# A window-attention layer's TensorE order written out part by part, with two smaller reorderings in the layers behind it

## The chip, the core and the metric

The kernel runs on one core of one Trainium2 chip. The metric is the device time of one execution in microseconds; lower is better. The core has TensorE for matrix products, with a weight load ahead of each (the profile lists the two as PE and PEld), VectorE (DVE), ScalarE (ACT), GpSimd (POOL) and SyncE (SP), which here only issues DMA transfers. Each engine takes its instructions in the order of its own queue and waits at semaphores for what other engines have to do first.

## The reference

Eight images of 56 x 56 pixels with 192 channels, in float32, go through four layers of one form: x becomes x + layer(GroupNorm(x)).

- Layer 0 is a gated unit with two Toeplitz products, along the rows and along the columns.
- Layer 1 is shifted-window attention. The image is rolled by 3 pixels and cut into 64 windows of 7 x 7 = 49 pixels. A layer norm is followed by q, k and v; each of 6 heads of 32 channels computes softmax(q k^T / sqrt(32) + bias + mask) v in each window; an output projection follows.
- Layer 2 projects 192 channels to 384, mixes the pixels of every channel with a banded matrix, takes running averages along image directions, and then applies a layer norm and a projection back to 192.
- Layer 3 is a depthwise convolution, a layer norm, and two projections with a hidden layer of 768 channels.

## The kernel before, in words

The kernel treats the layers one after the other, each as one stage or several. In layers 1 to 3 the 192 channels lie as 3 groups (j) of 64 on the partitions, and two halves of the image (s, rows 0 to 27 and 28 to 55) share the 128 partitions. Tile, the layer that the kernel is written in, keeps an order of its own for each engine: a planner reorders instructions within what the data allow, unless the program says otherwise. Three means of saying otherwise occur here: `tc.manual_schedule(engines=...)` keeps the named engines in program order from there to the end of the enclosing block, `tc.keep_in_program_order(...)` keeps single instructions in it, and a buffer count (`bufs`) makes an instruction wait until the older user of the buffer is done.

**Layer 1, units.** An image is worked in 4 units (g): 7 rows of pixels of each half, 8 windows in each half, 392 pixels a half. A unit has these steps, and the names in brackets are those of the profile:

- the projections of q and k (line 677, `qk_ps`): two for q, two for k, each of 6 matmuls into two banks; copied by ACT (683, 685) or DVE (687)
- v (line 697, `v_ps`): two groups of 4 windows, each 48 matmuls into two banks; copied by ACT for half 0 (705) and by DVE for half 1 (707)
- the scores (line 717, `S`): 48 matmuls for each half, into one tile S of three banks; then on DVE the bias (724) and the maximum (726), on POOL the subtraction (727), on ACT the exponential (728), on DVE the sum (730) and its reciprocal (731), on POOL the scaling (732). The result is `e`, in one of two sets
- the mix: 12 transposes of `e` for each half in 3 groups (747, `et_ps`), copied by ACT and DVE in turn (752, 754); 48 matmuls with v (760, `po`), copied by ACT and DVE (771, 773); three projections (779, `pr`), each added to x on DVE (784)

One matmul of float32 data appears as two passes in the profile's counts, so that a group of 48 shows as 96.

PSUM has 8 banks here: three of tag `mm`, shared by qk, v, po, pr and the norm's products, two of tag `et`, and three for S.

**Layer 1, the norm.** `layer1_norm` is a generator for the following image: it scales (ACT, line 636), takes the mean over the channels with a matmul (643), subtracts it (DVE, 645), squares (ACT, 647), sums with a matmul (651), takes the square root (ACT, 652, once per unit on 32 partitions), the reciprocal (DVE, 654), spreads it with a matmul (659) and multiplies (DVE, 661). It hands back control 14 times, and the loop over the units calls it some times for each unit (`plan`).

**Layer 1, order.** In the loop the scores of unit g + 1 are written before the mix of unit g. The planner orders all engines.

**Layer 2's input.** `layer2_image` clears the edge rows of a buffer on POOL (790, 791) and loads an image (793, 794), one of two buffers (`xpool`). `layer2_in` scales it in 3 instructions on DVE (803) into `xn`, POOL clears edges in it (801, 806, 807), and 174 passes on TensorE (815, `pin`) in 15 groups are each taken from PSUM by DVE with the bias (823). Image 0 is loaded by POOL's queue, the following ones by SyncE's.

**Layer 2's output and layer 3's input.** The layer norm's statistics (line 190), scalings (936 on DVE, 938 on ACT), transposes (947, `tp`), the affine part (948, ACT), the projection (960) and the addition to x (965, DVE) of one image lie beside `layer3_in` for the image before: its GroupNorm, transposes of the image (1006, `zps`) in 4 groups for each of 3 channel groups, and copies to `zt`, by DVE (995) and ACT (993) in turn, stored for the depthwise convolution. DVE runs in program order here.

Of the kernel before, what the change touches and what calls it, by code (L numbers as in the profile page):

```python
# [10 lines left out]
F32 = mybir.dt.float32  # L11
# [8 lines left out]
HC = 96  # L20
# [57 lines left out]
def kernel(ctx: ExitStack, tc: tile.TileContext, a: dict, out: bass.AP):  # L78
# [105 lines left out]
    def run(steps):  # L184
        for _ in steps:
            pass
# [435 lines left out]
    def layer1_norm(b, x, pool, psum, consts):  # L622
# [10 lines left out]
        for g in range(4):  # L633
            gs = bass.ts(g, TT)
            for j in range(3):
                nc.scalar.activation(
                    xw[:, j, gs].rearrange("p (w i j) -> p w i j", i=7, j=7),
                    x[:, j, 7 * g:7 * g + 7].rearrange("p i (w j) -> p w i j", j=7), AF.Identity,
                    bias=sh[:, j:j + 1], scale=sc[:, j:j + 1],
                )  # L640
            mp = psum.tile([128, 512], F32, name="mean", tag="mm", bufs=3)[:, 0:TT]
            for j in range(3):
                nc.tensor.matmul(mp, ones2, xw[:, j, gs], start=(j == 0), stop=(j == 2))
            xs = xw[:, :, gs]
            nc.vector.tensor_tensor(xs, xs, mp.unsqueeze(1).to_broadcast([128, 3, TT]), ALU.subtract)
            sq = pool.tile([128, 3, TT], F32, name="sq")
            nc.scalar.activation(sq, xs, AF.Square)
            yield
            vp = psum.tile([128, 512], F32, name="vps", tag="mm", bufs=3)[32 * g:32 * g + 32, 0:TT]
            for j in range(3):  # L650
                nc.tensor.matmul(vp, ones32, sq[:, j], start=(j == 0), stop=(j == 2))
            nc.scalar.activation(rs[32 * g:32 * g + 32], vp, AF.Sqrt, bias=eps5[32 * g:32 * g + 32])
            yield
        nc.vector.reciprocal(rs, rs)
        yield
        for g in range(4):
            gs = bass.ts(g, TT)
            bp = psum.tile([128, 512], F32, name="rstd", tag="mm", bufs=3)[:, 0:TT]
            nc.tensor.matmul(bp, sel[32 * g:32 * g + 32], rs[32 * g:32 * g + 32], start=True, stop=True)
            xs = xw[:, :, gs]  # L660
            nc.vector.tensor_tensor(xs, xs, bp.unsqueeze(1).to_broadcast([128, 3, TT]), ALU.mult)
            yield

    def layer1_scores(g, xr, pool, psum, S, es, consts):
# [5 lines left out]
        qk = [pool.tile([HC, 2, 2, TT], F32, name=f"qk{s}", bufs=1) for s in range(2)]  # L670
        for which in range(2):
            for m in range(2):
                ps = [psum.tile([128, 512], F32, name="qk_ps", tag="mm", bufs=3)[0:HC, 0:TT] for s in range(2)]
                c0 = which * C + m * HC
                for j in range(3):
                    for s in range(2):
                        nc.tensor.matmul(  # L677
                            ps[s], wg[64 * s:64 * s + 64, j, c0:c0 + HC], xw[64 * s:64 * s + 64, j, gs],
                            start=(j == 0), stop=(j == 2),
                        )  # L680
                for s in range(2):
                    if which == 0:
                        nc.scalar.activation(qk[s][:, 0, m], ps[s], AF.Identity, bias=bq[:, m:m + 1])  # L683
                    elif s == 0:
                        nc.scalar.copy(qk[s][:, 1, m], ps[s])
                    else:
                        nc.vector.tensor_copy(qk[s][:, 1, m], ps[s])

        v = [pool.tile([128, 8, HC], F32, name=f"v{s}") for s in range(2)]
        for w4 in range(0, 8, 4):  # L690
            ps = [psum.tile([128, 512], F32, name="v_ps", tag="mm", bufs=3)[:, 0:4 * HC] for s in range(2)]
# [10 lines left out]
            for s in range(2):  # L702
# [3 lines left out]
                else:  # L706
                    nc.vector.tensor_copy(dst, ps[s])
        for s in range(2):
            bm = pool.tile([128, 24, WN], F32, name="bm")
# [22 lines left out]
            nc.gpsimd.tensor_tensor(ev, ev, sm.unsqueeze(2).to_broadcast([128, 24, WN]), ALU.mult)  # L732
        return v

    def layer1_mix(g, x, v, pool, psum, es, consts):

        w_proj, bpr = consts[2:4]
        oa = []
        for s in range(2):
            e = es[g % 2][s]  # L740

            et = pool.tile([128, 12, 128], F32, name="et")
            for i in range(3):
                tp = psum.tile([128, 512], F32, name="et_ps", tag="et", bufs=2)
                for k in range(4):
                    at = 8 * i + 2 * k
                    nc.tensor.transpose(
                        tp[:, 128 * k:128 * k + 128], e[:, at:at + 2].rearrange("p a b -> p (a b)"), ident
                    )
                dst = et[:, 4 * i:4 * i + 4].rearrange("p a b -> p (a b)")  # L750
                if i % 2 == 0:
                    nc.scalar.copy(dst, tp)
                else:
                    nc.vector.tensor_copy(dst, tp)
            o = pool.tile([HC, 2, TT], F32, name=f"oa{s}", bufs=1)
            po = [psum.tile([128, 512], F32, name="po", tag="mm", bufs=3)[0:HC, 0:TT] for _ in range(2)]
# [10 lines left out]
            for hh in range(2):  # L767
# [4 lines left out]
                else:  # L772
                    nc.vector.tensor_copy(dst, src)
            oa.append(o)
        for j in range(3):
            ps = psum.tile([128, 512], F32, name="pr", tag="mm", bufs=3)[:, 0:TT]
# [6 lines left out]
            xs = x[:, j, 7 * g:7 * g + 7].rearrange("p i w -> p (i w)")  # L783
            nc.vector.scalar_tensor_tensor(xs, ps, bpr[:, j:j + 1], xs, ALU.add, ALU.add)


# [10 lines left out]
    def layer2_in(b, x, pool, psum, w_in, b_in):  # L797
# [4 lines left out]
        for j in range(3):  # L802
            nc.vector.tensor_scalar(
                xn[:, j, :, 0:W], x[:, j], sc[:, j:j + 1], sh[:, j:j + 1], ALU.mult, ALU.add
            )
        nc.gpsimd.memset(xn[0:64, :, 0, 0:W], 0.0)
# [161 lines left out]
    def layer3_in(b, x, zp, pool, psum):  # L968
# [21 lines left out]

        def to(dst, src, eng):
            if eng:
                nc.scalar.copy(dst, src)
            else:
                nc.vector.tensor_copy(dst, src)

        for j in range(3):
            zt = pool.tile([OP, 64, NB], F32, name="zt")
            nc.gpsimd.memset(zt[:, :, 0:1], 0.0)
            nc.gpsimd.memset(zt[:, :, NB - 1:NB], 0.0)  # L1000
            for g, m0 in enumerate(range(0, PH + 1, 4)):
                yield
# [10 lines left out]
                dst = bass.AP(dst.tensor, dst.offset, [list(dst.ap[0]), [1, n2], [PH, 2], [NB, 64]])  # L1013
                to(dst, tp[:, 0:n2], g % 2)
                if nm > n2:

                    to(zt[:, :, 1 + 2 * PH], tp[:, n2, 1], 0)
                    to(zt[0:64, :, 1 + PH], tp[0:64, n2, 0], 1)
            nc.sync.dma_start(zd[b][:, 64 * j:64 * j + 64], zt)
# [215 lines left out]
    with ExitStack() as st:  # L1235
# [25 lines left out]
        if nimg > 1:  # L1261
            x.append(layer1_load(1, xpool))
        values = layer1_scores(0, xr[0], pool, psum, S, es, consts)


        plan = [(1, 1, 1), (1, 1, 2), (1, 2, 1), (0, 1, 2)]
        gn = []
        last = slice(nimg - 1, nimg)
        for b in range(nimg):
            gn.append(pool.tile([128, 3, NTH, 6], F32, name="gh_st"))  # L1270
            steps = layer1_norm(b + 1, x[b + 1], pool, psum, consts) if b + 1 < nimg else iter(())
            for g in range(4):
# [6 lines left out]
                if g == 1 and b == nimg - 1:  # L1279
                    run(gn_finish(mv2[:, 0:b], scsh2[:, 0:b, 0], scsh2[:, 0:b, 1], pool, psum, "mm"))  # L1280
                first, second, third = plan[g]
                for _ in range(first):
                    ahead = next(steps, None)
                    if ahead is not None:
                        xr.append(ahead)
                for _ in range(second):
                    next(steps, None)
                following = None
                if g < 3 or b + 1 < nimg:
                    following = layer1_scores((g + 1) % 4, xr[b + (g == 3)], pool, psum, S, es, consts)  # L1290
                for _ in range(third):
                    next(steps, None)
                layer1_mix(g, x[b], values, pool, psum, es, consts)
                values = following
                gn_piece(gn[b], x[b].rearrange("p j h w -> p j (h w)"), g)
                if b + 1 == nimg:
                    rolled_rows(x2[b], x[b], g)
            for _ in steps:
                pass
            if b + 1 < nimg:  # L1300
# [5 lines left out]
    with ExitStack() as st:  # L1306
        xpool = st.enter_context(tc.tile_pool(reuse_waits="tile", name="l2x", bufs=2, side="right"))
        pool = st.enter_context(tc.tile_pool(reuse_waits="tile", name="l2i", bufs=2))
        psum = st.enter_context(tc.tile_pool(reuse_waits="tile", name="l2ip", bufs=4, space=PSUM))
        x = [layer2_image(0, xpool, nc.gpsimd)]  # L1310
        w_in = resident("w_in", nc.scalar, pool)
# [204 lines left out]
```

## Time and profile before

| what | value |
|---|---|
| time before, median of 3 runs (lowest, highest) | 6227.99 us (6226.70, 6247.08) |
| profiled execution: its own time | 6250.54 us |
| profiled execution: span, mean granted TensorE clock | 6248.8 us, 0.925 |
| busy in the span: PE, PEld | 5549.3 us (89%), 3585.7 us (57%) |
| busy in the span: DVE, ACT, POOL | 3450.3 (55%), 2251.5 (36%), 1328.0 (21%) |
| layer 1, from the first `mean` of image 1 to the last `pr` | about 2115 to 3568 us |
| layer 2's input | 3615.67 to 3859 us |
| layer 2's mixing, layer 2's output with layer 3's input | 3883 to 4490 us, 4490 to 5040 us |

Times in the text count from the start of the span of the profiled execution. In a line of groups the columns are the line of the source, the engine, the operation, out<-in by names, the sizes and the count; behind the first bar the busy time and the mean in ns of one; behind the second the idle time of the engine just ahead of these instructions and what ended most of it. A line of the timeline has the start, the length and the group, and in brackets the idle time just before it with what ended it. "Issue" is time in which the engine waited for nothing that the profile shows. The granted clock is a share of full speed.

### The profile page before, as it was taken

The numbers are of one execution on the slowest core, as the hardware profiler recorded it, in microseconds if no ns is written. First come the engines' busy times: TensorE is split into PE (matmuls) and PEld (weight loads), VectorE is DVE, ScalarE is ACT, GpSimd is POOL, SyncE is SP. The second block draws the span as 40 slices with busy tenths as digits, with TensorE's granted clock in tenths as the row PEclk, the third lists the DMA queues.
The fourth block names the chain that finished last, engine by engine and source line by source line (L and its number), as shares of the span: only waits on it lengthen the run. The fifth ranks groups of instructions, "written<-read, shape, count | busy, mean of one in ns | idle before, by whom it ended". The sixth has DMA issues, their size and how long they took to land. (4 is left out here: it accounts for less than half of the span.)

```text
span 6248.8 us, 126609 instructions
## 1 busy us (share of the span) xinstructions
PE 5549.3 (89%) x55636; PEld 3585.7 (57%) x55636; DVE 3450.3 (55%) x4800; ACT 2251.5 (36%) x2932; POOL 1328.0 (21%) x869
## 2 busy tenths in 40 slices
PE   6799989999999888888888688999888889799999
PEld 5577766666666454445444466767544479544444
DVE  5677766556565344444444376888788710433331
ACT  2334444344444233333333200445455510233333
POOL 1100025444444122121212101333300100110100
PEclk8899989999999888878888798999999989899999
DMA  6799986666665515545442586677667579421210
GB/s 165 186 216 214 191 242 255 264 261 258 256 256 213 80 34 60 60 60 56 56 48 41 67 239 226 209 232 239 189 167 208 162 288 331 154 82 64 72 57 24
DMA packets 1034540, 1013.11 MB, mean 162 GB/s; under 512 B 826136, under 2 KB 958196, under 8 KB 1007220
## 3 DMA queue, kind: packets, MB, share of 16 engines
q1 hardware_dynamic: 1019424, 940.93, 54.0%
q0 software_dynamic: 8832, 41.81, 2.2%
q10 hardware_dynamic: 5732, 22.27, 1.1%
q8 instruction: 437, 7.16, 0.5%
q14 instruction: 115, 0.94, 0.0%
HBM read 676.28 MB, written 345.08 MB: 163 GB/s over the span
## 5 line engine op out<-in xcount | busy, mean ns | idle before, releaser
L371 PE MATMUL qv<-w_qv_sb,xn 64*112 64x288 f32 x5376 | 722.1, 425 | 50.3 <-DVE act L377 46.9
L409 POOL COPY lc<-lt 128x896 f32<-128x896 f32 (+1 forms) x320 | 572.1, 1805 | 624.5 <-PE op L417 608.4
L371 PEld LDWEIGHTS qv<-w_qv_sb,xn 64*112 64x112 f32 x5376 | 535.0, 184 | 232.5 <-DVE act L377 63.2
L378 ACT ACTIVATE act<-act 112x576 f32<-112x576 f32 x448 | 299.9, 682 | 462.8 <-DVE act L377 425.8
L1145 PE MATMUL ph<-y,w_sb 64*128 64x392 f32 x2304 | 398.4, 498 | 6.5 <-ACT hid L1149 6.5
L429 PE MATMUL pj<-xn,w_p_sb 64*128 64x392 f32 (+1 forms) x1920 | 374.0, 516 | 14.0 <-issue 10.7
L1156 PE MATMUL po<-hid,w_sb 128*64 128x392 f32 x2304 | 386.3, 494 | 0.0
L417 PEld LDWEIGHTS op<-rc,lc 128*56 128x56 f32 x9216 | 310.6, 137 | 127.2 <-issue 61.8
L417 PE MATMUL op<-rc,lc 128*56 128x56 f32 x9216 | 342.1, 222 | 45.2 <-POOL lc L409 26.1
L450 PE MATMUL y<-pp,w_o_sb 128*64 128x392 f32 (+1 forms) x1920 | 357.3, 505 | 18.9 <-DVE x L458 10.2
L377 DVE TENSOR_TENSOR act<-qv,b_qv 112x576 f32<-112x576 f32 x448 | 320.7, 751 | 85.4 <-PE qv L371 85.0
L1163 DVE TENSOR_TENSOR x<-x,z 128x392 f32<-128x392 f32 x96 | 70.4, 733 | 522.8 <-ACT z L1161 522.8
L409 ACT COPY rc<-rt 128x896 f32<-128x896 f32 (+1 forms) x160 | 256.9, 1606 | 240.6 <-PE op L417 226.7
L727 POOL TENSOR_TENSOR e<-e,mx 128x1176 f32<-128x1176 f32 x64 | 139.9, 2185 | 954.3 <-DVE mx L726 899.4
L866 PE MATMUL cv<-zc,wt 128*128 128x224 f32 x1536 | 313.7, 356 | 24.1 <-DMA zc<-pd 24.1
L866 PEld LDWEIGHTS cv<-zc,wt 128*128 128x128 f32 x1536 | 290.9, 190 | 67.8 <-issue 51.6
L443 DVE TENSOR_TENSOR pp<-pp,ot 128x784 f32<-128x784 f32 (+1 forms) x160 | 154.6, 966 | 306.6 <-ACT pp L434 288.3
L677 PE MATMUL qk_ps<-xr,wg 64*96 64x392 f32 x1536 | 309.7, 512 | 15.1 <-ACT qk L683 13.5
L1145 PEld LDWEIGHTS ph<-y,w_sb 64*128 64x128 f32 x2304 | 220.4, 189 | 176.4 <-issue 26.0
L1046 PE MATMUL cps<-zc,wt 128*128 128x224 f32 x1536 | 299.5, 356 | 18.0 <-DMA zc<-zd 17.6
L1046 PEld LDWEIGHTS cps<-zc,wt 128*128 128x128 f32 x1536 | 289.5, 189 | 27.8 <-issue 20.4
L1156 PEld LDWEIGHTS po<-hid,w_sb 128*64 128x64 f32 x2304 | 162.6, 137 | 213.8 <-issue 213.8
(211 smaller groups left out, 9423.0 us busy)
## 6 DMA issues: line engine op xcount, KB each, us to landing
lt<-left SPq DMA_DIRECT2D x72, 1792.0 KB
rt<-right SPq DMA_DIRECT2D x72, 1792.0 KB
left<-qv SPq DMA_DIRECT2D x224, 252.0 KB
right<-qv SPq DMA_DIRECT2D x448, 126.0 KB
wt<-in_band_dram SPq DMA_DIRECT2D x23, 2048.0 KB
wt<-in_band_dram SPq DMA_DIRECT2D x11, 4096.0 KB
zc<-pd SPq DMA_DIRECT2D x187, 232.0 KB
pd<-pt SPq DMA_DIRECT2D x7, 5568.0 KB
```

Of the source, the lines that this page charges most:

```text
L371: nc.tensor.matmul(ps[s][:, which, 0:D1 // 2], xn[64 * s:64 * s + 64, j, bass.ts(i, 2 * W)], w_qv[64 * s:64 * s + 64, j, which, ns], start ...
L377: nc.vector.tensor_tensor(act, ps[s][:, :, 0:D1 // 2], b_qv[:, :, ns], ALU.add)
L378: nc.scalar.activation(act, act, AF.Silu)
L409: copy(c[:, 0:nu], raw.rearrange("p (w u d) -> p u d w", u=nu, d=64 // nu)[:, :, d0:d0 + 8])
L417: nc.tensor.matmul(op[64 * u:64 * u + W, i, :], lc[:, u, i], rc[:, u, i], start=True, stop=True)
L429: nc.tensor.matmul(ps[0:M, s, 0:TT], w_p[64 * s:64 * s + 64, j, d0:d0 + M], xn[64 * s:64 * s + 64, j, ts], start=(j == 0), stop=(j == 2),)
L450: nc.tensor.matmul(y[64 * s:64 * s + 64], w_o[0:M, c, 64 * j:64 * j + 64], pp[0:M, s], start=(c == gated[0][0]), stop=(c == gated[-1][0]),)
L677: nc.tensor.matmul(ps[s], wg[64 * s:64 * s + 64, j, c0:c0 + HC], xw[64 * s:64 * s + 64, j, gs], start=(j == 0), stop=(j == 2),)
L866: nc.tensor.matmul(dst, wt[:, c4 + i, 128 * q:128 * q + 128], zc[:, :, c4 + i, q:q + NPAIR], start=(q == 0), stop=(q == 1),)
L1046: nc.tensor.matmul(dst.rearrange("p (b n) -> p b n", n=NPAIR), wt[:, c4 + i, q * OP:(q + 1) * OP], zc[:, :, c4 + i, q:q + NPAIR], start=(q ...
L1145: nc.tensor.matmul(ps[:, s, 0:TT], w0[64 * s:64 * s + 64, j, m * 128:(m + 1) * 128], y[64 * s:64 * s + 64, j, ts], start=(j == 0), stop=(j ...
L1156: nc.tensor.matmul(ps[64 * s:64 * s + 64], w1[:, m, 64 * j:64 * j + 64], hid[:, m, s], start=(m == 0), stop=(m == 5),)
```

## The change

Layer 1's norm: for each unit the generator now hands back control behind the scaling and behind the square, and then ahead of each spreading matmul: 13 stops in place of 14. The variances are copied from PSUM by DVE, one unit after the other, and one square root over 128 partitions follows.

Layer 1's unit: `layer1_scores` and `layer1_mix` return lists of closures in place of writing their instructions at once: Q (four projections of q and k), V (two), E (two score parts, each with its softmax), T (six groups of transposes), P (two mixes with v) and R (three projections). The loop takes them in the order of a plan of 24 entries, N standing for the next step of the norm; Q, V and E are of unit g + 1, the others of unit g. TensorE is kept in program order in this stage; DVE, ACT and POOL are still ordered by the planner. The first unit's parts are written ahead of the loop in the order Q, E, V, E, V.

Layer 2's input: the scalings are kept in program order on DVE, and image 0 is loaded by ACT's queue.

Layer 3's input: all copies to `zt` go to ACT.

```diff
 layer1_norm
                     bias=sh[:, j:j + 1], scale=sc[:, j:j + 1],
                 )
+            yield
             mp = psum.tile([128, 512], F32, name="mean", tag="mm", bufs=3)[:, 0:TT]
...
-            nc.scalar.activation(rs[32 * g:32 * g + 32], vp, AF.Sqrt, bias=eps5[32 * g:32 * g + 32])
+            nc.vector.tensor_copy(rs[32 * g:32 * g + 32], vp)
+        nc.scalar.activation(rs, rs, AF.Sqrt, bias=eps5)
+        nc.vector.reciprocal(rs, rs)
+        for g in range(4):
             yield
-        nc.vector.reciprocal(rs, rs)
-        yield
-        for g in range(4):
...
-            yield
 layer1_scores: the bodies become project(which, m), values(w4), weights(s)
-        return v
+        return v, [
+            [lambda which=which, m=m: project(which, m) for which in range(2) for m in range(2)],
+            [lambda w4=w4: values(w4) for w4 in (0, 4)], [lambda s=s: weights(s) for s in range(2)],
+        ]
 layer1_mix: the bodies become turn(s, i), mix(s), project(j)
+        return [
+            [lambda s=s, i=i: turn(s, i) for s in range(2) for i in range(3)],
+            [lambda s=s: mix(s) for s in range(2)], [lambda j=j: project(j) for j in range(3)],
+        ]
 the loop of layer 1
-        values = layer1_scores(0, xr[0], pool, psum, S, es, consts)
-        plan = [(1, 1, 1), (1, 1, 2), (1, 2, 1), (0, 1, 2)]
+        values, (Q, V, E) = layer1_scores(0, xr[0], pool, psum, S, es, consts)
+        for part in Q + [E[0], V[0], E[1], V[1]]:
+            part()
+        plan = "T T Q N T T Q T P N T Q N Q P E N V E N V R R R".split()
+        st.enter_context(tc.manual_schedule(engines={mybir.EngineType.PE}))
...
+                for kind in plan:
+                    if kind == "N":
+                        next(steps, None)
+                    elif parts.get(kind):
+                        parts[kind].pop(0)()
 layer2_in
-            nc.vector.tensor_scalar(
+            tc.keep_in_program_order(nc.vector.tensor_scalar(
                 xn[:, j, :, 0:W], x[:, j], sc[:, j:j + 1], sh[:, j:j + 1], ALU.mult, ALU.add
-            )
+            ))
 layer3_in
-                to(dst, tp[:, 0:n2], g % 2)
+                nc.scalar.copy(dst, tp[:, 0:n2])
                 if nm > n2:
-                    to(zt[:, :, 1 + 2 * PH], tp[:, n2, 1], 0)
-                    to(zt[0:64, :, 1 + PH], tp[0:64, n2, 0], 1)
+                    nc.scalar.copy(zt[:, :, 1 + 2 * PH], tp[:, n2, 1])
+                    nc.scalar.copy(zt[0:64, :, 1 + PH], tp[0:64, n2, 0])
 layer 2's input stage
-        x = [layer2_image(0, xpool, nc.gpsimd)]
+        x = [layer2_image(0, xpool, nc.scalar)]
```

More of the change, by code (lines that the diff above doesn't have):

```diff
@@ L670, in layer1_scores, with project, values @@
         qk = [pool.tile([HC, 2, 2, TT], F32, name=f"qk{s}", bufs=1) for s in range(2)]
[L671 to L679, printed above, removed]
-                        )
-                for s in range(2):
[L682 to L690, printed above, removed]
+        v = [pool.tile([128, 8, HC], F32, name=f"v{s}") for s in range(2)]
+        def project(which, m):
+            ps = [psum.tile([128, 512], F32, name="qk_ps", tag="mm", bufs=3)[0:HC, 0:TT] for s in range(2)]
+            c0 = which * C + m * HC
+            for j in range(3):
+                for s in range(2):
+                    nc.tensor.matmul(
+                        ps[s], wg[64 * s:64 * s + 64, j, c0:c0 + HC], xw[64 * s:64 * s + 64, j, gs],
+                        start=(j == 0), stop=(j == 2),
+                    )
+            for s in range(2):
+                if which == 0:
+                    nc.scalar.activation(qk[s][:, 0, m], ps[s], AF.Identity, bias=bq[:, m:m + 1])
+                elif s == 0:
+                    nc.scalar.copy(qk[s][:, 1, m], ps[s])
+                else:
+                    nc.vector.tensor_copy(qk[s][:, 1, m], ps[s])
+        def values(w4):
             ps = [psum.tile([128, 512], F32, name="v_ps", tag="mm", bufs=3)[:, 0:4 * HC] for s in range(2)]
@@ L707, in layer1_scores, with weights @@
                     nc.vector.tensor_copy(dst, ps[s])
-        for s in range(2):
+        def weights(s):
             bm = pool.tile([128, 24, WN], F32, name="bm")
@@ L732, in layer1_scores, with turn, mix @@
             nc.gpsimd.tensor_tensor(ev, ev, sm.unsqueeze(2).to_broadcast([128, 24, WN]), ALU.mult)
-        return v
+        return v, [
+            [lambda which=which, m=m: project(which, m) for which in range(2) for m in range(2)],
+            [lambda w4=w4: values(w4) for w4 in (0, 4)], [lambda s=s: weights(s) for s in range(2)],
+        ]
     def layer1_mix(g, x, v, pool, psum, es, consts):
         w_proj, bpr = consts[2:4]
[L738 to L755, printed above, removed]
+        ets = [pool.tile([128, 12, 128], F32, name="et") for _ in range(2)]
+        oa = [pool.tile([HC, 2, TT], F32, name=f"oa{s}", bufs=1) for s in range(2)]
+        def turn(s, i):
+            e, et = es[g % 2][s], ets[s]
+            tp = psum.tile([128, 512], F32, name="et_ps", tag="et", bufs=2)
+            for k in range(4):
+                at = 8 * i + 2 * k
+                nc.tensor.transpose(
+                    tp[:, 128 * k:128 * k + 128], e[:, at:at + 2].rearrange("p a b -> p (a b)"), ident
+                )
+            dst = et[:, 4 * i:4 * i + 4].rearrange("p a b -> p (a b)")
+            if i % 2 == 0:
+                nc.scalar.copy(dst, tp)
+            else:
+                nc.vector.tensor_copy(dst, tp)
+        def mix(s):
+            et, o = ets[s], oa[s]
             po = [psum.tile([128, 512], F32, name="po", tag="mm", bufs=3)[0:HC, 0:TT] for _ in range(2)]
@@ L773, in layer1_mix, with project @@
                     nc.vector.tensor_copy(dst, src)
-            oa.append(o)
-        for j in range(3):
+        def project(j):
             ps = psum.tile([128, 512], F32, name="pr", tag="mm", bufs=3)[:, 0:TT]
@@ L802, in layer2_in @@
         for j in range(3):
-            nc.vector.tensor_scalar(
+            tc.keep_in_program_order(nc.vector.tensor_scalar(
                 xn[:, j, :, 0:W], x[:, j], sc[:, j:j + 1], sh[:, j:j + 1], ALU.mult, ALU.add
-            )
+            ))
         nc.gpsimd.memset(xn[0:64, :, 0, 0:W], 0.0)
@@ L989, in layer3_in @@
         yield
[L991 to L995, printed above, removed]
         for j in range(3):
@@ L1000, in layer3_in @@
             nc.gpsimd.memset(zt[:, :, NB - 1:NB], 0.0)
-            for g, m0 in enumerate(range(0, PH + 1, 4)):
+            for m0 in range(0, PH + 1, 4):
                 yield
@@ L1262 @@
             x.append(layer1_load(1, xpool))
-        values = layer1_scores(0, xr[0], pool, psum, S, es, consts)
-        plan = [(1, 1, 1), (1, 1, 2), (1, 2, 1), (0, 1, 2)]
+        values, (Q, V, E) = layer1_scores(0, xr[0], pool, psum, S, es, consts)
[3 more added lines that the diff above has]
+        st.enter_context(tc.manual_schedule(engines={mybir.EngineType.PE}))
+        last = slice(nimg - 1, nimg)
         gn = []
-        last = slice(nimg - 1, nimg)
         for b in range(nimg):
             gn.append(pool.tile([128, 3, NTH, 6], F32, name="gh_st"))
-            steps = layer1_norm(b + 1, x[b + 1], pool, psum, consts) if b + 1 < nimg else iter(())
+            steps = iter(())
+            if b + 1 < nimg:
+                steps = layer1_norm(b + 1, x[b + 1], pool, psum, consts)
+                xr.append(next(steps))
             for g in range(4):
@@ L1280 @@
                     run(gn_finish(mv2[:, 0:b], scsh2[:, 0:b, 0], scsh2[:, 0:b, 1], pool, psum, "mm"))
[L1281 to L1288, printed above, removed]
-                if g < 3 or b + 1 < nimg:
[L1290 to L1294, printed above, removed]
+                parts = dict(zip("TPR", layer1_mix(g, x[b], values, pool, psum, es, consts)))
+                if g < 3 or b + 1 < nimg:
+                    values, of_next = layer1_scores((g + 1) % 4, xr[b + (g == 3)], pool, psum, S, es, consts)
+                    parts.update(zip("QVE", of_next))
+                for kind in plan:
[3 more added lines that the diff above has]
+                        parts[kind].pop(0)()
                 gn_piece(gn[b], x[b].rearrange("p j h w -> p j (h w)"), g)
@@ L1297 @@
                     rolled_rows(x2[b], x[b], g)
-            for _ in steps:
-                pass
+            run(steps)
             if b + 1 < nimg:
```

## The prediction, made before the changed kernel ran

> **What bounds the kernel now.** I read the page's slices first: TensorE is busy for 89% of the span, so a change is worth what it does to TensorE's idle time and clock in the stages that it touches. The windows by stage give both (columns: stretch and length, busy us of PE, PEld, DVE, ACT, POOL, granted clock, DMA):
> ```profile
> 2500.00:2700.00 200.00, 166.30 (x3181) 98.76 (x3177) 91.42 (x111) 68.73 (x101) 37.11 (x18) 0.85 0.45 56
> 3616.00:3859.00 243.00, 242.04 (x1420) 169.85 (x1418) 195.58 (x144) 0.26 (x1) 14.92 (x33) 0.97 0.68 224
> 4490.00:5040.00 550.00, 439.62 (x2416) 233.36 (x2416) 412.59 (x764) 280.95 (x398) 59.56 (x79) 0.90 0.63 179
> ```
> Layer 1 (first row, about 2115 to 3568) leaves 17% idle at clock 0.85. Layer 2's input (second) has no idle time: anything put on its path costs in full. Layer 2's output (third) has idle time at DVE's hands. For layer 1 the groups on TensorE over 2440 to 3340, with what ended their idle time:
> ```profile
> L677 PE MATMUL qk_ps<-xr,wg 64*96 64x392 f32 x960 | 190.3, 506 | 9.9 <-ACT qk L683 8.8
> L697 PE MATMUL v_ps<-wg,xr 64*64 64x96 f32 x3840 | 101.9, 247 | 16.4 <-issue 10.7 <-ACT v L705 4.0
> L747 PE MATMUL et_ps<-ident,e 128*128 128x128 f32 x486 | 98.7, 345 | 38.1 <-ACT et L752 22.7 <-POOL e L732 12.6 <-issue 2.2
> L760 PE MATMUL po<-et,v 49*32 49x49 f32 x4032 | 76.7, 252 | 30.9 <-DVE et L754 16.7 <-issue 10.7 <-DVE oa L773 2.8
> L651 PE MATMUL vps<-sq,ones 128*32 128x392 f32 x126 | 60.6, 631 | 28.0 <-ACT sq L647 28.0
> L717 PE MATMUL S<-qk 32*49 32x49 f32 x3840 | 59.2, 223 | 16.4 <-issue 14.0 <-DVE e L724 1.8
> ```
> With pr's 4.0 that is 144 us in 900; images take 177.4, 174.3 and 178.3 us (first qk of group 1 at 2186.43, 2363.79, 2538.08, 2716.35), mean 176.7, so 28.3 us idle an image: 7.4 issue, 20.9 waits for other engines.
>
> The softmax chain decides the new order (S end to exponential, then sum and scaling):
> ```profile
> L724 DVE TENSOR_TENSOR e<-S,bm 128x1176 f32<-128x1176 f32 x40 | 55.3, 1382 | 37.9 <-PE S L717 26.9 <-PE et_ps L747 8.7 <-remote 2.3
> L726 DVE TENSOR_REDUCE mx<-e 128x24 f32<-128x1176 f32 x40 | 54.9, 1372 | 1.6
> L727 POOL TENSOR_TENSOR e<-e,mx 128x1176 f32<-128x1176 f32 x41 | 89.6, 2186 | 554.5 <-DVE mx L726 499.6 <-PE vps L651 36.0 <-PE et_ps L747 9.5
> L728 ACT ACTIVATE e<-e 128x1176 f32<-128x1176 f32 x41 | 49.6, 1209 | 85.7 <-POOL e L727 85.5
> ```
>
> **Layer 1: the work.** Warm durations from the timeline: a T (8 passes) 1.05, a Q 2.37, a V 2.5, an E 1.25, a P 1.33, an R 1.52. So 6 T + 4 Q + 2 V + 2 E + 2 P + 3 R = 6.3 + 9.5 + 5 + 2.5 + 2.7 + 4.6 = 30.5 us a unit; the norm adds 4 x (2.24 mean + 2.16 vps + 0.9 rstd) = 21.2 an image: 143.2. The change leaves this alone. Before, 143.2 + 28.3 idle leaves 176.7 - 171.5 = 5.2 us an image for the low clock.
>
> **Layer 1: the waits.** T parts no longer stand in a row and norm steps lie between other parts, so the et, po and vps waits above mostly go. What comes late is at the end: E V E V R R R, with three mm banks for all. TensorE's order is fixed; DVE and ACT keep the planner's, and in the built program ACT has each V copy behind the exponential of the same half, DVE has the second half's bias addition behind the first half's sum. From the end of E0 the exponential ends at 1.38 + 1.37 + 2.19 + 1.21 + four hand-overs of 0.07 = 6.45. V0, E1, V1 keep TensorE until 6.25. R0 needs the bank of ACT's V0 copy: 6.98. R1 needs the bank of DVE's V1 copy, behind sum (1.37), reciprocal (0.3), bias addition, maximum (1.38, 1.37) and itself (0.56): 11.5, though R0 ends at 8.5. R2 needs ACT's V1 copy, behind the second exponential: 15.0, against 13.0. Waits 0.7 + 3.0 + 2.0, and 0.5 each ahead of the last Q and of P1: 6.8 in a unit without norm steps beside E (groups 2 and 3). In groups 0 and 1 norm steps fill that place: about 3.5 (vps on its square 1.7, P1 0.8, the rest small) and 3.1 (R0 behind the rstd product). Sum 6.8 + 6.8 + 3.5 + 3.1 = 20.2 against 20.9: the waits move, they hardly shrink.
>
> Square roots: 4 become one, with 4 DVE copies (about 0.6 each). L652's and L728's table loads are 21 each at 1.283 us; from 8 an image they fall to about 2, some 8 us of ACT, on an engine busy 34%. ACT's late answers are by order, not load, so nothing is booked; if ACT were the bound, it would be at most 6 x 1.28 = 7.7 an image.
>
> **Layer 1: issue and clock.** As many small matmuls are issued; their bursts are cut by Q and N, but at the end V and E still adjoin. Of 7.4 I take 5.5, between half and all; bounds 0 and 7.4. The granted clock is only 0.50 or 1.00 in 2-us windows: 0.50 from about 2479.4 to 2492.6 and 2520.8 to 2534.0, 13.2 us each, about one a unit, on po, et and pr. In the new order a low stretch after the waits of R1 and R2 lies on R2 and the next T T Q N T T Q, and Q is all streaming: up to 6.6 lost. Two units of four have such waits, so 13.2, less what the waits in between absorb: 10 (0 to 26). The image: 143.2 + 20.2 + 5.5 + 10 = 178.9, +2.2 on before, over 8 images +17. Bounds: 163.4 (-106) and 197.2 (+164).
>
> The Trainium skill ("TensorE: Matmul & The Clock Gate", "HAM oscillation") puts the fall of the clock at idle gaps above about 3.4 us. The first fall above follows a single gap of 0.94 us amid small matmuls, and against that row the rule is too lenient. By the rule layer 1's 3.0-us waits would keep it warm (80 us less than my sum), and image edges of layer 2, next, would cool it.
>
> **Layer 2's input.** DVE scales one image ahead today, out of images' order:
> ```profile
> 3610.03 6.48 DVE L803 TENSOR_SCALAR xn<-x,scsh 128x1680 f32<-128x1680 f32 x6 [40.30 <-DMA x<-x]
> ...
> 3646.88 0.85 DVE L823 TENSOR_TENSOR pt<-pin,b_in_sb 128x384 f32<-128x384 f32 x1 [0.39 <-PE pin L815]
> 3647.57 3.26 DVE L803 TENSOR_SCALAR xn<-x,scsh 128x1680 f32<-128x1680 f32 x3
> 3650.74 5.68 DVE L823 TENSOR_TENSOR pt<-pin,b_in_sb 128x768 f32<-128x768 f32 x4
> ```
> ```profile
> 3615.67 176.30 PE L815 MATMUL pin<-w_in_sb,xn 64*128 64x384 f32 x1044 [47.62 <-POOL xn L806]
> ```
> The scalings at 3647.57 are image 2's while TensorE works on image 1: six images without a gap. In the built program after, image b+1's three scalings stand behind image b's last eviction. At each of 7 edges TensorE waits 0.38 + 0.69 (eviction) + 3.26 (scalings) + 0.06 + 0.23 (POOL's memset) + 0.05 = 4.7. Behind a gap of this length work is slow: zps x8 took 1.94 after 4.64 idle and 1.07 after 1.17 (below), +0.9; the first pin group after 47.62 took 4.14 for 1.94, +2.2. So 5.6 (up to 6.9) x 7 = +39 (33 to 48). The cover gone is DVE's look-ahead.
>
> The 47.62 gap: before, image 0's scalings wait with image 1's load (landed 3610.0). After, image 0's load goes out on ACT's queue, behind b_in's and behind stores of the last unit (the last landed at 3595.49), issued about 3590 to 3594.5; with the 10.9 and 17.7 us of before it lands near 3605 to 3610, and POOL's memset for image 0 stands behind one that waits for those stores. Start 3611.5: -4. Bounds 0, and -19 (start just behind the stores, 3596.6).
>
> **Layer 2's output.** DVE is busy without a break 4725 to 4764 of each 61.6-us image, and TensorE waits for its zt copies:
> ```profile
> 4747.22 1.07 PE L1006 MATMUL zps<-ident,zp 128*128 128x128 f32 x8 [1.17 <-DVE zt L995]
> ...
> 4759.62 1.94 PE L1006 MATMUL zps<-ident,zp 128*128 128x128 f32 x8 [4.64 <-DVE zt L995]
> ```
> All go to ACT, idle there. Four stretches of L995 (4740.93, 4746.03, 4752.02, 4758.41; 0.9 to 1.05 net each) leave DVE's path: 3.8 x 7 = -27; ACT's own crowded stretch (4760 to 4772) gets one copy more, about 0.5 x 8 = +4. Net -23 (-35 to 0): the statistics (L190, 0.8 each) still fill DVE, so it stays the bound and no more comes.
>
> **Sum.** +17 + 39 - 4 - 23 = +29: 6250.5 to 6279.5 for the profiled execution, which lay 22.5 above the median of the runs; by the median, 6228 + 29 = 6257.
>
> **The rivals.** *A, forecast:* layer 1 within about 4 us an image, edges lost: 6215 to 6300. *B, faster:* layer 1's fixed order keeps the clock at 1.00 and its bursts fed. For it: 20.9 + 7.4 + 5.2 us an image are there to take, and the largest waits (et 38.1, po 30.9, vps 28.0) are those it spreads. Against: the V copies behind the exponential. With 163.4 an image it gives -106 + 12 = -94, 6134; it decides from 172 an image down (-38, and the total -26). *C, slow clock:* all four units drop the clock onto Q and R: 197 an image, +164 + 12, 6400; half of that 6316. *D, the change doesn't do what it says:* images in order but nothing earlier at the start, or the edges hidden by banks still to be evicted: edges 0 to 15, total about 0.
>
> Chances: A 0.50 (0.33 slower, 0.14 within 0.3%, 0.03 faster), B 0.30, C 0.14, D 0.06 (0.04 within, 0.01 each side). 0.3%, 19 us, is what a measurement of this kernel tells from none. Faster 0.34, within 0.18, slower 0.48. The range leaves out the lower third of B and the upper half of C: 6165 to 6345.
>
> **What would show it.** Right: R waits for v copies of ACT and DVE, 3 and 2 us in groups 2 and 3; et and vps waits down to a few us; seven gaps of 4 to 6 us ahead of pin, ended by POOL's memset; zps waiting for ACT alone. Wrong: layer 1's images under 172 us with a clock above 0.9, or over 185 with Q at twice 2.37; no gaps in layer 2's input; its first matmul under 30 us behind layer 1's last.

## The result, and the profile after

The changed kernel takes 6123.68 us (6119.55 to 6129.09), against 6227.34 for the kernel before in the same series: a ratio of 0.9827 with a 95% interval of 0.9810 to 0.9844, 104 us less. The forecast was 6257 us with a range from 6165; the time lies below it. The profiled execution took 6119.55 us, its span 6117.8, at a mean granted clock of 0.943 (before 0.925).

The same stages in the windows of the kernel after (busy us of PE, PEld, DVE, ACT, POOL, clock, DMA):

```profile
2500.00:2700.00 200.00, 170.82 (x3310) 102.21 (x3306) 99.09 (x131) 64.75 (x102) 42.34 (x21) 0.93 0.57 64
3469.00:3757.00 288.00, 255.73 (x1420) 148.77 (x1420) 201.71 (x148) 0.26 (x1) 14.63 (x34) 0.92 0.61 197
4380.00:4930.00 550.00, 449.57 (x2458) 232.95 (x2457) 368.65 (x695) 323.30 (x471) 61.10 (x80) 0.90 0.67 195
```

In layer 1 (first row) the share of busy time hardly moved (83% to 85%), but the clock did: 0.85 to 0.93. Layer 2's input (second row) now has 32 us without work in 288.

From the first and last pass of each stage (lengths in us; a last pass is counted to its start):

| profiled execution | layer 1, first qk to last pr | gap to pin | pin | first tp to first depthwise matmul |
|---|---|---|---|---|
| before, as in the prediction | 1403.7 | 48.1 | 242.8 | 535.8 |
| after | 1276.7 | 30.7 | 286.4 | 515.3 |
| `before_again` | 1379.5 | 45.0 | 242.8 | 535.4 |
| `l1_only` | 1267.8 | 41.1 | 242.7 | 535.4 |
| `l2in_only` | 1386.8 | 30.6 | 287.4 | 534.9 |
| `zt_only` | 1382.7 | 45.4 | 242.6 | 517.9 |

The groups on TensorE in layer 1 (2300 to 3200), with what ended the idle time before them:

```profile
L698 PE MATMUL v_ps<-wg,xr 64*64 64x96 f32 x4416 | 125.8, 269 | 22.8 <-issue 22.4 <-ACT v L706 0.4
L788 PE MATMUL pr<-oa,w_proj_sb 96*64 96x392 f32 x552 | 112.8, 547 | 38.1 <-ACT v L706 23.6 <-DVE xr L662 9.1 <-DVE v L708 5.3
L754 PE MATMUL et_ps<-ident,e 128*128 128x128 f32 x548 | 83.5, 291 | 0.0
L719 PE MATMUL S<-qk 32*49 32x49 f32 x4329 | 75.3, 217 | 56.0 <-issue 55.3
L769 PE MATMUL po<-et,v 49*32 49x49 f32 x4286 | 59.3, 210 | 12.9 <-ACT qk L687 7.9 <-ACT qk L685 5.0
```

The waits of et (38.1 before) and vps (28.0) are gone, po's fell from 30.9 to 12.9. In their place stand pr's 38.1 for v copies and rstd products, and issue waits of 78.5 us, twice those of before. In all 134 us in 900, where 144 were. What fell clearly is the mean length of a pass of three groups: pr from 641 to 547 ns, et from 345 to 291, po from 252 to 210. V's rose from 247 to 269 and the norm's mean products' from 510 to 583.

Layer 2's input, on TensorE and then on DVE:

```profile
3469.83 31.55 PE L830 MATMUL pin<-w_in_sb,xn 64*128 64x384 f32 x174 [30.22 <-POOL xn L821]
3505.71 30.68 PE L830 MATMUL pin<-w_in_sb,xn 64*128 64x384 f32 x174 [4.33 <-POOL xn L821]
```
```profile
3501.42 0.84 DVE L838 TENSOR_TENSOR pt<-pin,b_in_sb 128x384 f32<-128x384 f32 x1 [0.39 <-PE pin L830]
3502.11 3.26 DVE L818 TENSOR_SCALAR xn<-x,scsh 128x1680 f32<-128x1680 f32 x3
3509.41 1.54 DVE L838 TENSOR_TENSOR pt<-pin,b_in_sb 128x768 f32<-128x768 f32 x1 [4.05 <-issue]
```

The scalings follow the last eviction, and each image starts 4.3 us after the one before, with a slow beginning (30.7 to 32.2 us an image for 29.0).

In layer 2's output the waits of zps have gone (4330 to 4870; 42.4 us for DVE's copies and 8.9 for ACT's before), and DVE's scalings are what is late next:

```profile
PE tp L962 <- DVE yt L951: 57.9, 16, 16.9
...
PE zps L1015 <- ACT zt L1023: 1.4, 5, 0.3
```

### The profile page after: what moved, and what is told of

Same layout as the page of the kernel before. It is cut to its first block, busy times and chain, and to the rows that moved or that the text cites. A ratio compares the mean times of both kernels' runs of the same rounds, so it can differ in the third digit from the quotient of the medians.

```text
span 6117.8 us, 126576 instructions
## 1 busy us (share of the span) xinstructions
PE 5451.9 (89%) x55636; PEld 3509.4 (57%) x55636; DVE 3401.5 (56%) x4760; ACT 2216.8 (36%) x2938; POOL 1330.2 (22%) x867
## 5 line engine op out<-in xcount | busy, mean ns | idle before, releaser
L417 PE MATMUL op<-rc,lc 128*56 128x56 f32 x9216 | 339.4, 221 | 43.9 <-POOL lc L409 25.7
L881 PE MATMUL cv<-zc,wt 128*128 128x224 f32 x1536 | 312.8, 355 | 24.2 <-DMA zc<-pd 24.2
L830 PE MATMUL pin<-w_in_sb,xn 64*128 64x384 f32 x1392 | 251.5, 511 | 60.4 <-POOL xn L821 60.4
```

The source lines that it names most:

```text
L417: nc.tensor.matmul(op[64 * u:64 * u + W, i, :], lc[:, u, i], rc[:, u, i], start=True, stop=True)
L881: nc.tensor.matmul(dst, wt[:, c4 + i, 128 * q:128 * q + 128], zc[:, :, c4 + i, q:q + NPAIR], start=(q == 0), stop=(q == 1),)
```

## The experiments

Times are compared by ratios within a series, since the kernel before took 6206 to 6214 us in the later ones. Each ratio has its 95% interval.

**The parts alone.** `l1_only` is the kernel before with layer 1's edits; `l2in_only` has those of layer 2's input and `zt_only` those of layer 3's input; `before_again` is the kernel before.

> The kernel before with the change to layer 1 alone (norm, parts, fixed TensorE order). Theory A, from the two traces: layer 1 from its first qk to its last pr falls from 1404 to 1277 us, and the time with it, to about 6100 to 6120. Theory B, the forecast's sum: layer 1 is 17 us longer, 6245, and the gain of the changed kernel came from elsewhere.

> The kernel before with the change to layer 2's input alone (scalings in program order on DVE, image 0 loaded by ACT's queue). Theory A, from the two traces: seven gaps of 4.3 us and slow starts behind them cost 44 us, the earlier start brings 17 back: 26 us slower, about 6253. Theory B, the forecast: 39 lost, 4 won, 6263. A rival: the earlier start of after comes from layer 1's different end, not from the queue; then the gap ahead of pin stays at 47 us and the time is 6271.

> The kernel before with all zt copies on ACT, alone. Both theories expect the stretch from the first tp of layer 2's output to the first matmul of the depthwise convolution to fall from 536 to about 513 to 516 us, 20 to 23 us, time 6205. A rival: part of the 20.5 us between the two traces is chance; then under 10 us.

> The kernel before once more, for a second profile: the first profiled execution lay 22 us above the median of the runs. If the 22 us lie in layer 1, its length from first qk to last pr is nearer to 1380 than to 1404, and the gain of layer 1 is nearer to 105 than to 127.

Measured: `l1_only` 0.9823 (0.9805 to 0.9842), -110 us; `l2in_only` 1.0050 (1.0027 to 1.0072), +31; `zt_only` 0.9971 (0.9959 to 0.9983), -18. The sum is -1.56%, where the whole change has -1.73%; the intervals cover the difference. `before_again`, 6219.9 us, has 24 us less in layer 1 than the first profile of the kernel before: that much of the 127 us between the first two traces is chance, and layer 1's gain is about 103 to 112. So the whole result is layer 1's, and the other two edits add up to some 13 us of loss. The table above places each part in its own stage. In `l2in_only` the gap ahead of pin falls to 30.6 us with layer 1 as before, so the earlier start doesn't come from layer 1's different end.

**What in layer 1.** `planner_order` drops the line that fixes TensorE's order, and the parts are still written in the same sequence; `grouped_order` keeps the line and groups the parts; `four_roots` undoes the single square root.

```diff
 planner_order
-        st.enter_context(tc.manual_schedule(engines={mybir.EngineType.PE}))
 grouped_order
-        plan = "T T Q N T T Q T P N T Q N Q P E N V E N V R R R".split()
+        plan = "N Q Q Q Q V V N E E N T T T P T T T P N R R R N".split()
 four_roots
-            nc.vector.tensor_copy(rs[32 * g:32 * g + 32], vp)
-        nc.scalar.activation(rs, rs, AF.Sqrt, bias=eps5)
+            nc.scalar.activation(rs[32 * g:32 * g + 32], vp, AF.Sqrt, bias=eps5[32 * g:32 * g + 32])
```

> The changed kernel without the line that fixes TensorE's order in layer 1: parts are written in the same sequence, the planner orders TensorE too. Theory A1 (the fixed order does it, by fewer low-clock stretches): layer 1 back at 1350 to 1390 us with clock 0.86 and 0.998 of the time before. Rival A2 (one square root and the sequence of writing do it, which also move DVE and ACT): layer 1 stays at 1270 to 1290 us, ratio 0.983.

> The changed kernel with a fixed order that groups the parts instead of alternating them: N Q Q Q Q V V N E E N T T T P T T T P N R R R N. Theory A1 in its sharper form (alternating is what matters): waits for et and po copies stand in a row again, clock 0.86 or lower, layer 1 at 1350 to 1450 us. Rival A3 (any fixed order does it): 1270 to 1300 us.

> The changed kernel with four square roots of 32 partitions on ACT for each image, as before, in place of four DVE copies and one root. If table loads count: some 6 more for each image, 1.28 us each on ACT, behind which copies wait; layer 1 longer by 20 to 60 us. If they lie in ACT's idle time: within 10 us of the changed kernel's 1268 to 1277 us.

Measured: `planner_order` 0.9858 (0.9843 to 0.9872), `grouped_order` 1.0053 (1.0036 to 1.0071), `four_roots` 0.9827 (0.9811 to 0.9842). The sequence in which the parts are written does nearly all of it: left to the planner, TensorE takes much the same order, and layer 1 takes 1279.4 us against 1276.7. A fixed order by itself brings nothing, and the norm's new stops, which `grouped_order` keeps, bring nothing either: grouped, the kernel is 33 us slower than before, some 20 more than the 13 that the other two edits lose. The single root is worth nothing in time, although the table loads fell from 42 in 900 us to 10. The windows over 2165 to 3400 of `before_again`, `grouped_order` and `planner_order`:

```profile
2165.00:3400.00 1235.00, 1048.87 (x19648) 615.15 (x19647) 571.77 (x710) 447.83 (x651) 253.12 (x122) 0.87 0.35 52
```
```profile
2165.00:3400.00 1235.00, 1028.38 (x19034) 608.21 (x19033) 568.01 (x723) 379.46 (x578) 244.42 (x118) 0.85 0.35 51
```
```profile
2165.00:3400.00 1235.00, 1061.21 (x21177) 639.44 (x21175) 614.71 (x799) 400.72 (x630) 271.00 (x130) 0.91 0.40 57
```

Between the last two, busy time differs by 3%, the count of passes done in it by 11%: a pass takes less time, and the clock is 0.91 in place of 0.85.

**The waits that the forecast worried about.** `v_among_t` moves V between the T parts and R between the scores; `v_one_earlier` puts each V one place earlier (together with `scale_midway`, below).

```diff
-        plan = "T T Q N T T Q T P N T Q N Q P E N V E N V R R R".split()
 v_among_t
+        plan = "Q T T Q N T T Q V T P N T Q N V P N E R E N R R".split()
 v_one_earlier
+        plan = "T T Q N T T Q T P N T Q N Q V P E N V N E R R R".split()
```

> The changed kernel with another order of parts: Q T T Q N T T Q V T P N T Q N V P N E R E N R R, v away from the exponentials and R between the scores. If R's waits for v copies (28.9 us in 2300 to 3200) and the issue waits in the burst of E and V (78.5 us there) go by such spreading: layer 1 shorter by 40 to 120 us, ratio 0.963 to 0.976, clock above 0.94. Rival: the issue waits come with the number of small matmuls and only move, and T waits for POOL's scaling of e instead: 1260 to 1300 us, ratio 0.98 to 0.985.

> The kernel of scale_midway with each V one place earlier: T T Q N T T Q T P N T Q N Q V P E N V N E R R R. The first v copies now stand ahead of both exponentials and the second behind the first one only. If R's waits for v copies cost what they take in the trace: some 30 of 38 us in 900 go, about 40 us over layer 1 (1268 to about 1230), ratio 0.970. Rival, from v_among_t: the waits go, but the scaling of e is late for T and the low clock falls on the following Q, layer 1 at 1260 to 1300 us, ratio 0.975 to 0.983.

Measured: `v_among_t` 0.9899 (0.9882 to 0.9916), layer 1 1309.9 us; `v_one_earlier` 0.9909 (0.9892 to 0.9925), layer 1 1357.6 us. Both lie beyond the 1300 us that the rivals allowed. Both were meant to be faster and were slower than the order of the change. In `v_one_earlier` R's waits went as meant and came back at the transposes:

```profile
L788 PE MATMUL pr<-oa,w_proj_sb 96*64 96x392 f32 x528 | 112.0, 583 | 1.9 <-issue 1.9
L754 PE MATMUL et_ps<-ident,e 128*128 128x128 f32 x506 | 84.5, 300 | 65.6 <-POOL e L734 61.3 <-ACT et L759 4.2
```

With V moved away from the scores, the chain from the second E to the scaled e has less TensorE work beside it, and T waits for POOL. In the order of the change, V and R's waits lie where e is being made anyway. `v_among_t` does cut idle time (169 us in layer 1, 193 in the kernel after), and is slower all the same: its clock is 0.88 where the kernel after has 0.92, and the passes of Q and R take 570 and 617 ns in the mean where they took 505 and 547:

```profile
L679 PE MATMUL qk_ps<-xr,wg 64*96 64x392 f32 x1056 | 251.8, 570 | 38.8 <-DVE x L793 32.8 <-DVE rs L653 5.9
L788 PE MATMUL pr<-oa,w_proj_sb 96*64 96x392 f32 x528 | 125.6, 617 | 0.4 <-DVE e L726 0.4
```

**The clock by itself.** `dense_in_waits` adds dense work where R waits.

```diff
-        plan = "T T Q N T T Q T P N T Q N Q P E N V E N V R R R".split()
+        plan = "T T Q N T T Q T P N T Q N Q P E N V E N V R W R W R".split()
+                    elif kind == "W":
+                        wp = psum.tile([128, 512], F32, name="warm", tag="et", bufs=2)[:, 0:TT]
+                        for _ in range(2):
+                            nc.tensor.matmul(wp, ones2, consts[0][:, 0, 0:TT], start=True, stop=True)
```

> The changed kernel with two more matmuls (128 x 128 with 392 columns, into an et bank that nobody reads), 1.45 us at full clock, ahead of each unit's second and third R, where TensorE waits for v copies. If the low clock sets layer 1's time and dense work ends or prevents it: low-clock time in layer 1 falls, clock above 0.94, layer 1 shorter by 10 to 60 us in spite of 93 us of added work, or at least not longer by more than 10. If the clock is only a by-product: 31 units x 2.9 us less the waits covered, layer 1 longer by 10 to 90 us.

Measured: 0.9899 (0.9885 to 0.9914); layer 1 1302.4 us, 26 to 34 longer than without it (1276.7 after, 1268.2 in `scale_midway`). The expectation of a gain failed: the added work costs more than it saves, and the result lies in the 10 to 90 us that were written down for a clock that is only a by-product. So this run doesn't show by itself that the clock sets layer 1's time. Its groups:

```profile
L788 PE MATMUL pr<-oa,w_proj_sb 96*64 96x392 f32 x544 | 108.0, 519 | 10.4 <-DVE xr L662 7.8 <-ACT v L706 1.9 <-DVE v L708 0.5
...
L1307 PE MATMUL warm<-wg,ones 128*128 128x392 f32 x184 | 74.8, 530 | 0.0
```

The clock did move as expected. By the trace's clock records over 2165 to 3400, low-clock time fell from 190 to 154 us, and pr's mean from 547 to 519 ns.

**What layer 1 consists of.** Let the low clock's loss be (1 - clock) x length, that is, half of the time at clock 0.50. If all low-clock time were busy and every pass took twice as long in it, busy time less this loss would be the full-clock work, the same in every kernel that does the same:

| kernel | layer 1 | PE busy | idle | clock | loss | busy less loss |
|---|---|---|---|---|---|---|
| `before_again` | 1379.5 | 1171.2 | 208 | 0.86 | 193 | 978 |
| `grouped_order` | 1403.5 | 1165.5 | 238 | 0.85 | 211 | 955 |
| after | 1276.7 | 1083.2 | 193 | 0.92 | 102 | 981 |
| `planner_order` | 1279.4 | 1097.0 | 182 | 0.91 | 115 | 982 |
| `four_roots` | 1253.8 | 1081.3 | 172 | 0.92 | 100 | 981 |
| `v_among_t` | 1309.9 | 1141.1 | 169 | 0.88 | 157 | 984 |
| `v_one_earlier` | 1357.6 | 1114.3 | 243 | 0.89 | 149 | 965 |
| `dense_in_waits` | 1302.4 | 1167.9 | 134 | 0.93 | 91 | 1077 |

It nearly is: 978 to 984 in five kernels, 955 and 965 in the two with most idle time, and 1077 with added work of 93; rounding of the clock leaves some 7 us open in each row. Of the 103 us between `before_again` and after, 91 are the low clock's loss by this measure and some 15 idle time.

The measure is rather an upper bound, though. By the clock records 63 of the 387 us at low clock were idle in `before_again`, and 26 of 206 after. And small matmuls don't take twice as long. Two runs of 88 passes of po in the kernel before, the first at a clock of 0.50, the second at 1.00:

```profile
2484.79 1.52 PE L760 MATMUL po<-et,v 49*32 49x49 f32 x88
2569.89 1.04 PE L760 MATMUL po<-et,v 49*32 49x49 f32 x88
```

An estimate prices every pass at the mean that its kind takes in the same trace where the clock is 1.00. By it the low clock costs 140 us in `before_again` and 85 after, 56 of the 103. The remaining 32 are then time at full clock: four Q in a row took 9.48 us at clock 1.00 before (at 2459.75), and one Q between other parts takes 2.22 after; two V took 4.99 (at 2469.16), and one takes 2.2 after. So the low clock is the largest part of the gain, between 56 and 91 us by these two accounts; no run separates it from the rest.

**Layer 2's input.** `scale_midway` writes image b + 1's scalings and memsets behind the eighth group of image b; `no_scale_order` leaves scalings to the planner.

```diff
 scale_midway: layer2_in split into layer2_scale (scalings, memsets) and the groups
             nc.vector.tensor_tensor(dst, ps[:, 0:ns, 0:C2], b_in[:, v, 0:ns], ALU.add)
+            if i == nh // 2:
+                ahead()     # layer2_scale(b + 1, ...), if there is one
 no_scale_order
-            tc.keep_in_program_order(nc.vector.tensor_scalar(
+            nc.vector.tensor_scalar(
```

> The changed kernel with image b+1's scalings (and their memsets) written midway through image b's groups in layer 2's input, still in program order on DVE. If the edges of 4.3 us and the slow starts behind them come from the scalings' place alone: pin takes 243 to 248 us in place of 286, the gap ahead of it stays at 30, ratio 0.975 to 0.977. Rival: DVE (1.55 of each 1.94 us in use) cannot take 3.3 us more within an image without holding TensorE up: pin 255 to 270.

> The changed kernel with the scalings left to the planner; image 0 still goes out on ACT's queue. If the queue brought the gap ahead of pin down from 45 to 30: it stays at 30, and pin falls from 286 towards 243, with perhaps 10 us at the start where evictions wait behind image 1's scalings; ratio about 0.977. If the order on DVE brought it down: the gap is back at 41 to 45, ratio about 0.979.

Measured: `scale_midway` 0.9767 (0.9752 to 0.9781), 6062.61 us beside 6205.84 of the kernel before: faster than the kernel before and the changed one. pin takes 241.5 us, six images without a gap:

```profile
3456.94 176.50 PE L834 MATMUL pin<-w_in_sb,xn 64*128 64x384 f32 x1044 [29.58 <-POOL xn L821]
```

`no_scale_order` 0.9791 (0.9775 to 0.9807): the two expected ratios lie too close to decide, and the measured one is nearer to that of the order on DVE. The trace decides: the gap ahead of pin stays at 30.2, so image 0's queue closed it and not the order on DVE. pin takes 251.0 us. One stall is left at the start, where evictions stand behind image 1's scalings, which wait for its load:

```profile
3467.33 10.32 PE L830 MATMUL pin<-w_in_sb,xn 64*128 64x384 f32 x48 [29.77 <-POOL xn L821]
3483.49 169.43 PE L830 MATMUL pin<-w_in_sb,xn 64*128 64x384 f32 x996 [5.84 <-DVE pt L838]
```

## Why the prediction was wrong

**The step that failed** is the price of the low clock in layer 1 before: 5.2 us an image, taken as what was left of 176.7 after 143.2 of work and 28.3 idle. The work was too large, and mostly by one term: a T was counted at 8 passes and 1.05 us, where it has 4. The kernel writes 4 transposes for a T, each of them one pass: line 754 has 768 passes in 8 images of 4 units with 6 T each. After, `T T` is what takes 1.09 us, at a clock of 1.00:

```profile
2444.67 1.09 PE L754 MATMUL et_ps<-ident,e 128*128 128x128 f32 x8
2445.70 2.22 PE L679 MATMUL qk_ps<-xr,wg 64*96 64x392 f32 x12
...
2451.87 0.66 PE L754 MATMUL et_ps<-ident,e 128*128 128x128 f32 x4
```

At 1.03 us from `T T` to the start of Q, six T are 3.1 us a unit and not 6.3, which is 12.8 us an image (an estimate from these rows). Smaller shares come from lengths that overlap the next group by the tail of their last matmul (a Q is 2.22 long, and its follower starts after 2.15, where 2.37 was booked), and from V at 2.5. By the table full-clock work is some 980 us over layer 1, 123 an image. What the work had too much, the remainder had too little. A bound on the loss could be read from the first row that the prediction shows: clock 0.85, 15% of 176.7 us, 26.5 an image. The two stretches at clock 0.50 that the prediction names say the same: 13.2 us in about every unit is 6.6 lost, 26 an image, and not 5.2. By `before_again` it is at most 193 / 8 = 24, and 17.5 by the estimate pass by pass.

The other side was about right. For the order after the forecast had 25.7 us an image of waits and issue and 10 of low clock; measured are 24.2 and, at most, 12.8. (The upper bound of an image adds up to 196.8, not 197.2; nothing hangs on it.) So the comparison was 35.7 against 33.5 where by the table it is 37 against 50 (26.0 idle and 24.1 low clock). The sign of being wrong that the prediction named came: images of 156.5 to 165.4 us at a clock above 0.9.

**The walk of the waits** held in kind: R waits for the v copies of ACT and DVE, idle time hardly shrinks (208 to 193 us). Its shares were off. In the trace R's second and third wait 1.6 and 1.9 us, not 3.0 and 2.0, and pr's waits come to 6.8 us an image; issue waits rose to 14 where 5.5 were booked. They lie ahead of the last V's end, and time lost there is not lost again at R.

**Rival B** named the mechanism that the clock would rise. That its 6134 us were near is luck: it supposed a clock of 1.00 and bursts that are fed, where the clock is 0.92 and the bursts starve more, and the work that it took too large makes up for both.

**Layer 2's input, the edges:** right. 4.33 us each, 43.6 in all by the two profiles against 39. DVE's look-ahead was the cover, and `scale_midway` gives it back.

**Layer 2's input, the start:** -14 to -17 us, where -4 was forecast with a bound of -19. The step that failed was that image 0's load would go out 22 to 26 us behind the last pr. The rows of ACT's queue and of POOL after (last pr ends at 3439.62):

```profile
3451.16 0.69 ACTq L807 DMA_DIRECT2D x<-x  x1
```
```profile
3466.49 0.77 POOL L804 MEMSET x<- 64x168 f32 x1 [34.19 <-DMA x<-x]
...
3469.55 0.23 POOL L821 MEMSET xn<- 64x168 f32 x1 [0.95 <-DVE xn L818]
```

It went out after 11.5 us. POOL's memsets behind the stores, which the bound supposed to hold the start, end at 3468.60. POOL then waits 0.95 us for DVE's scalings of image 0, which run from 3465.93 to 3469.49 behind its load: the load and the scalings hold the start, by about 1 us.

**Layer 2's output:** right; -18 to -20.5 against -23, and DVE is still what is waited for.

## What to carry to other kernels

Read a bound on what a low clock costs from the granted clock itself, (1 - clock) x time, before any sum is made; a price that is left over from a sum takes up every error in the other terms. Check each term of the sum against the count of passes, too: 768 passes of T would have shown the double booking. Idle time that is moved rather than removed can still pay. Alternating small and dense parts brought the gain here, but two other alternating orders, `v_among_t` and `v_one_earlier`, lost about a third and most of it; so run the orders, and compare busy time and clock, not waits alone. Whoever keeps an engine in program order should look for the work that it did ahead of order, and write that work earlier.

## What the runs showed of the hardware

The granted clock in the trace's records is 0.50 or 1.00 and nothing else. Low-clock stretches in layer 1 are about as many before as after, 37 and 40 in the two profiles before and 38 after over 2165 to 3400, but before they last up to 20.5 and 23.9 us (359 and 331 us in all), after up to 10.2 (190). They come in multiples of 3.4 us. The Trainium skill ("TensorE: Matmul & The Clock Gate", "What's actually happening") tells of a free-running activity window of about 3.4 us, which agrees. Its limit for idle gaps does not: in the kernel after, the clock falls at 2423.1 behind a gap of 2.2 us amid small matmuls (second row: the clock, 0.50, stands third from the end).

```profile
2422.39 0.42 PE L719 MATMUL S<-qk 32*49 32x49 f32 x20 [2.20 <-issue]
2424.00:2426.00 2.00, 2.00 (x4) 0.35 (x2) 0.29 (x1) 0.00 (x0) 0.00 (x0) 0.50 0.32 52
```

That long stretches before lie on et, po and pr, and short ones after have Q or the norm's matmuls close behind, fits dense work as what ends them; which kinds of matmul count as activity was not tried, so this part is argued, not shown.

Issue waits depend on the place of the small matmuls, not only on their number: 37.6 us in 900 before, 78.5 after, 32 in `v_among_t` with the same matmuls.
